# Recurrent mixing: value rows spread by transfers from DRAM, products and scans in SBUF

## The chip, the cores and the metric

The kernel runs on one core of one Trainium2 chip. The core has five engines that matter here: TensorE (PE, with its weight loads as PEld), VectorE (DVE), ScalarE (ACT), GpSimd (POOL) and SyncE (SP), which mostly issues DMAs. Each engine runs its own instruction stream in order, and the streams are tied together by semaphores. The metric is device time in microseconds (us) of one execution, as the median of several runs.

## What is computed

The reference runs four layers, one after the other, on 8 batch entries of 256 positions and 512 channels, all in float32: an attention block over two inputs (L0), a recurrent mixing block with 32 heads of 16 channels (L1), a decoder block with self-attention, cross-attention and an MLP (L2), and a non-local block of 1x1 convolutions (L3). The change is in L1, in its recurrence:

```python
def step(s, inp):
    k_l, v_l, w_l, r_l = inp
    a = k_l[..., :, None] * v_l[..., None, :]
    out = jnp.einsum('bhs,bhst->bht', r_l, faaaa * a + s)
    s_new = a + w_l[..., None] * s
    return (s_new, out)
```

Each head keeps a state of 16 x 16 numbers. At every position the state is multiplied by a decay w per key channel, the outer product of k and v is added, and the state is read out with r: multiplied and summed over the 16 key channels. The term with faaaa needs no state and is worked out apart (`bonus`). Ahead of the recurrence, k, v, r, w and a gate g come from projections of a mixed and normalised input; after it come a normalisation of each head, the gate, an output projection, and a second mixing block (`cm_` functions) of three projections.

## The kernel before

The program has four stretches: L0, the recurrent mixing of all eight entries, the self- and cross-attention of all entries, and the MLP with L3. The recurrent mixing is written in the class `Middle`. Its work is of two kinds.

The first kind is the recurrence, cut into 64 steps: 8 entries (b), 4 tiles of 128 channels (ct), 2 halves of the value channels (hf). In one step the 128 partitions hold 8 heads with 16 key channels each, and the free dimension holds 8 value channels of 256 positions each. The recurrence along the positions is one scan instruction over rows of 256; the decay of column 0 in each row is zero, so that a row starts from the initial state written there. A step consists of

- `spread` (L895): the value rows lie 128 channels to a partition. Eight matmuls with a selection matrix (`esel`, L902) copy the eight value rows of each head to the 16 partitions of that head, shifted by one position, into `vb`, which takes four banks of PSUM and has one buffer.
- `states` (L907): DVE copies the initial state to column 0 (L921), multiplies `vb` by k in two halves (L924), both in PSUM, and scans each half (L928) with the decays `w4`, which ACT writes for every second step (L912, L913). The scan reads `vb` from PSUM and `w4` from SBUF and writes a new SBUF tile `a`. POOL multiplies `a` by r into another tile `rs` (L933).
- `gather` (L936): eight matmuls with a selection matrix (`gsel`, L945) sum `rs` over the key channels into `yp`, one bank of PSUM; after the second half DVE adds the bonus (L951).

The second kind is everything else of the mixing, for the next entry and the one before: norms, projections, `mixed` (L762, whose DVE lines L777 read PSUM and whose POOL lines L784 add in SBUF), the shift (L737, with L741 and L744 on DVE), `head_norm`, `gated` (POOL L866), `gate` (DVE L876), `cm_` functions (POOL L971, L976, L995). These pieces are filler: the tables `steps` and `after` (L1199, L1210) give each function a due time in units of steps, eight to an entry, and `Filler.until` runs all that are due. The loop that joins both kinds is

```python
for n, at in enumerate(every):
    states(*at)
    fill.until(n + 0.95)
    if n:
        gather(*every[n - 1])
    fill.until(n + 0.99)
    if n + 1 < len(every):
        spread(*every[n + 1])
```

In this stretch only PE's stream is kept in the order of the program; the other engines' streams are ordered by the framework's scheduler, unless an instruction is pinned (`keep_in_program_order`). Matmul results of the filler go through a ring of PSUM banks (`mm`, L713), three in this stretch. Weights (1 MB for each of eight matrices, fetched anew for each entry by `load`, L809) come through a ring of SBUF buffers; their DMAs are issued by SP and wait there until the buffer is free.

Later lines that the text speaks of: `masked` (L1132) takes the attention tiles `pe`, from the same SBUF ring (tag "a") as the recurrence; `turn` (L1165) writes them to DRAM and reads them back with DMAs of 128 KB (L1177). In the MLP, sums of weights and activations are made on DVE and POOL, from SBUF to SBUF (L1351 to L1354 and L1360 to L1363), and results are combined from PSUM (L1407 to L1418).

Of the kernel before, what the change touches and what calls it, by code (L numbers as in the profile page):

```python
# [16 lines left out]
P = 128  # L17
# [76 lines left out]
def rows_of(halves):  # L94

    return [halves[k // 2][:, k % 2, :] for k in range(CT)]
# [20 lines left out]
def stage_l0(g, pools):  # L117
# [494 lines left out]

    "esel": (4, P), "gsel": (4, 32),
    "bfa": (CT, P),
# [7 lines left out]
class Middle:  # L622
# [62 lines left out]
    def plan(self):  # L685
        g, cp, wpool = self.g, self.cp, self.wpool
        nc, I = g.nc, g.I
        HS, NG = 16, 4
        w1, w2, w2g, d1, d2, s0, bones, bmean, cmean, esel, gsel, bfa = self.c.values()

# [28 lines left out]

        t_ = {}  # L720

        def fetch(b, tag, bufs):
            x = t_[tag, b] = wk.tile([P, ST, D], F32, tag=tag, name=tag, bufs=bufs)
            nc.sync.dma_start(out=x, in_=g.x1[b])

# [83 lines left out]
        def load(b, W):  # L809
            t_[W, b] = rows_of(g.weight(wpool, I["l1" + W + "T"], name=W))  # L810

# [80 lines left out]

        vbs, rss, w4s, yps = {}, {}, {}, {}

        def spread(b, ct, hf):  # L895

            v_ = t_["v", b]
            vb = vbs[b, ct, hf] = ps.tile([P, NG, 2, S], F32, tag="vb", name="vb", bufs=1)
            for j in range(2):
                for n in range(NG):  # L900
                    r = slice(32 * n, 32 * n + 32)
                    nc.tensor.matmul(  # L902
                        vb[:, n, j, 1:S], lhsT=esel[r, 2 * hf + j, :], rhs=v_[r, ct, 0 : S - 1],
                        start=True, stop=True,
                    )

        def states(b, ct, hf):  # L907


            if hf == 0:  # L910
                w4 = w4s[b, ct] = wk.tile([P, 4, S], F32, tag="w4", name="w4")
                nc.scalar.memzero(w4[:, :, 0:1])  # L912
                nc.scalar.activation(  # L913
                    w4[:, :, 1:S], t_["w", b][:, ct : ct + 1, 0 : S - 1].to_broadcast([P, 4, S - 1]),
                    AF.Exp, scale=-1.0,
                )
            w4 = w4s[b, ct]
            kb = t_["k", b][:, ct : ct + 1, 0 : S - 1].to_broadcast([P, 4, S - 1])
            rb = t_["r", b][:, ct : ct + 1, :].to_broadcast([P, 4, S])
            vb = vbs.pop((b, ct, hf)).rearrange("p n j l -> p (n j) l")  # L920
            nc.vector.tensor_copy(vb[:, :, 0], s0[:, b, ct, hf])  # L921
            for n2 in range(2):
                h = vb[:, 4 * n2 : 4 * n2 + 4, 1:S]
                nc.vector.tensor_tensor(h, h, kb, ALU.mult)  # L924
            rss[b, ct, hf] = []
            for n2 in range(2):
                a = wk.tile([P, 4, S], F32, tag="a", name="a", bufs=6)
                nc.vector.tensor_tensor_scan(  # L928
                    a.rearrange("p n l -> p (n l)"), w4.rearrange("p n l -> p (n l)"),
                    vb[:, 4 * n2 : 4 * n2 + 4, :].rearrange("p n l -> p (n l)"), 0.0, ALU.mult, ALU.add,  # L930
                )
                rs = wk.tile([P, 4, S], F32, tag="a", name="rs", bufs=6)
                nc.gpsimd.tensor_tensor(rs, a, rb, ALU.mult)  # L933
                rss[b, ct, hf].append(rs)

        def gather(b, ct, hf):  # L936
            if hf == 0:
                yps[b, ct] = ps.tile([P, S], F32, tag="y", name="yp", bufs=1)
                if ct % 2 == 0:
                    t_["y", b, ct // 2] = wk.tile([P, 2, S], F32, tag="y", name="y", bufs=2)  # L940
            yp = yps[b, ct]
            rs2 = rss.pop((b, ct, hf))
            for j in range(2):
                for n in range(NG):
                    nc.tensor.matmul(  # L945
                        yp[32 * n : 32 * n + 32, :], lhsT=gsel[:, 2 * hf + j, :],
                        rhs=rs2[n // 2][:, 2 * (n % 2) + j, :],
                        start=(hf == 0 and j == 0), stop=(hf == 1 and j == 1),
                    )
# [47 lines left out]
        def store(b):  # L997
            g.x2[b] = g.dram([P, ST, D], f"x2_{b}")
            nc.sync.dma_start(out=g.x2[b], in_=t_.pop(("xo", b)))


        HD, NH = 32, 4
        runs = [(pre, b) for pre in ("a_", "c_") for b in range(B)]

        pin = lambda ins: self.tc.keep_in_program_order(ins)

# [125 lines left out]
        def masked(i, ct, h2):  # L1132


            pe = t_["pe", i, ct, h2] = wk.tile([P, 2 * ST, S], F32, tag="a", name="pe", bufs=6)
            nmax = t_["nmax", i, ct, h2] = sm.tile([P, 2 * ST], F32, tag="nmax", name="nmax", bufs=4)
# [42 lines left out]
        def values(i, ct):  # L1179
# [92 lines left out]
        def loop(psums):  # L1272
            every = [(b, ct, hf) for b in range(B) for ct in range(CT) for hf in range(2)]
            bufs[0] = 3
            fill.until(-0.001)
            spread(*every[0])
            for n, at in enumerate(every):
                states(*at)
                fill.until(n + 0.95)
                if n:  # L1280
                    gather(*every[n - 1])
                fill.until(n + 0.99)
                if n + 1 < len(every):
                    spread(*every[n + 1])
            gather(*every[-1])
# [394 lines left out]
def host_layout(i):  # L1680
# [23 lines left out]
    vo = np.arange(D).reshape(CT, 8, 16).transpose(0, 2, 1).reshape(-1)  # L1704
    for nm in ("Wv", "Wg"):
        a["l1" + nm + "T"] = a["l1" + nm + "T"][:, vo]
    a["l1WoT"] = a["l1WoT"][vo]
    for nm in ("maa_w1", "decay_w1", "decay_w2"):
        a[nm] = L1[nm]
    w2 = L1["maa_w2"]  # L1710
# [4 lines left out]
    s0 = c[:, 2:18].reshape(B, CT, P, 4, 2, 2).transpose(2, 0, 1, 4, 3, 5)  # L1715
    a["s0"] = s0.reshape(P, B, CT, 2, 8)
    hs, th = np.arange(P) // 16, np.arange(P) % 8
    a["bones"] = (hs[:, None] == th[None, :]).astype(f)
# [3 lines left out]
    a["esel"] = np.stack([((t4 == t)[:, None] & (th[:, None] == hs[None, :])) for t in range(4)], 1).astype(f)  # L1722
    a["gsel"] = np.stack([((t4 == t)[None, :32] & (hs[:, None] == th[None, :32])) for t in range(4)], 1).astype(f)
    for nm in ("w_qkv", "w_ao", "w_q", "w_kv", "w_co", "w1", "w2"):
# [5 lines left out]
        "gn_w": L1["gn_w"][vo], "gn_b": L1["gn_b"][vo],  # L1730
        "bo": L0["bo"], "rwb": L0["r_w_bias"], "faaaa": L1["faaaa"],
        "a_ln_s": L2["ln1_s"], "a_ln_b": L2["ln1_b"], "c_ln_s": L2["ln2_s"], "c_ln_b": L2["ln2_b"],
# [36 lines left out]
```

## Time and profile before

| | us |
|---|---|
| median of 3 runs | 3414.48 (3413.72 to 3415.98) |
| the profiled execution | 3407.23 |
| its span in the profile | 3405.5 |
| first to last matmul of `spread` (L902) | 1377.2 to 2150.2 |
| PE busy over the span | 3197.5 (94%) |
| DVE busy | 2408.6 (71%) |
| ACT busy | 1591.4 (47%) |
| POOL busy | 1664.1 (49%) |

The profile is that of one execution, taken by the hardware profiler. A group line gives the source line, the engine, the operation, the tile written and the tiles read, and the number of instructions. A line's own view gives the shortest, median and longest duration in ns, and then the first and last start in us. Busy time counts an instruction from its recorded start to its end, so time in which a started instruction waits for something inside the chip is in it. Idle time is put down to whatever released the engine. "PEclk" or "clock" is the share of the full TensorE clock that was granted. A table by stretch gives, for each stretch of the span, its length, the busy time of PE, PEld, DVE, ACT and POOL with their numbers of instructions, the granted clock, the DMA engines' busy share and GB/s.

### The profile page before, as it was taken

Reading aid. Unit: us, or ns where it says so; the run is one execution under the profiler, and the core shown is the slowest. Engines: PE = TensorE matmul, PEld = TensorE weight load, DVE = VectorE, ACT = ScalarE, POOL = GpSimd, SP = SyncE. Lnnn points to the kernel's source line nnn. Section 1 sums busy time; section 2 is a strip of 40 time slices with the busy share of each in tenths; the row PEclk is TensorE's granted clock in tenths of the full one; section 3 lists DMA queues with packets and bytes.
Section 4 is the critical chain, followed back from the end, with each engine's and each line's share of the span. In section 5 each row is a group of like instructions: output and inputs, shape, how many; then the busy total and the mean of one; then the engine's idle time right before and its main releaser. Section 6 shows DMA issues by size and latency. Waiting matters only on the chain. (4 is left out here: it accounts for less than half of the span.)

```text
span 3405.5 us, 68751 instructions
## 1 busy us (share of the span) xinstructions
PE 3197.5 (94%) x26496; PEld 2271.7 (67%) x26496; DVE 2408.6 (71%) x4175; ACT 1591.4 (47%) x3983; POOL 1664.1 (49%) x1776
## 2 busy tenths in 40 slices
PE   8999999999999998889999998899989997899999
PEld 6777777777777765656666655555555553789996
DVE  4666666666666664787787887667868886677771
ACT  3555555555555553224334333566656664323223
POOL 6633233333333232455666665444434444688872
PEclk9999999999999998989999999899999998999999
DMA  7666566656657542312323233366777777400002
GB/s 269 228 202 198 189 192 194 204 184 196 207 176 223 173 128 69 112 55 87 106 93 111 95 101 101 106 231 238 252 247 256 267 258 245 164 1 1 1 13 87
DMA packets 273141, 533.08 MB, mean 157 GB/s; under 512 B 25056, under 2 KB 147312, under 8 KB 268720
## 3 DMA queue, kind: packets, MB, share of 16 engines
q1 hardware_dynamic: 251616, 456.48, 41.3%
q10 hardware_dynamic: 20528, 70.39, 5.4%
q8 instruction: 211, 3.46, 0.4%
q0 software_dynamic: 672, 1.81, 0.2%
q14 instruction: 114, 0.93, 0.1%
HBM read 411.15 MB, written 117.44 MB: 155 GB/s over the span
## 5 line engine op out<-in xcount | busy, mean ns | idle before, releaser
L391 POOL TENSOR_SCALAR pe<-pe,rinv 128x512 f32<-128x512 f32 x256 | 176.9, 691 | 609.1 <-DVE rinv L390 603.9
L368 DVE TENSOR_REDUCE nmax<-sp 128x2 f32<-128x1024 f32 x256 | 308.8, 1216 | 177.2 <-PE sp L363 177.2
L933 POOL TENSOR_TENSOR rs<-a,r 128x1024 f32<-128x1024 f32 x128 | 302.6, 2380 | 254.1 <-DVE a L928 223.1
L1161 POOL TENSOR_SCALAR pe<-pe,rinv 128x256 f32<-128x256 f32 x512 | 235.3, 478 | 349.6 <-DVE rinv L1159 345.2
L1151 ACT ACTIVATE pe<-pe,nmax 128x256 f32<-128x256 f32 x512 | 255.1, 499 | 210.5 <-DVE nmax L1142 204.4
L377 ACT ACTIVATE pe<-sp,nmax 128x512 f32<-128x512 f32 x512 | 347.0, 683 | 11.2
L403 DVE STREAM_TRANSPOSE pt<-pe 128x1024 f32<-128x1024 f32 x256 | 312.6, 1231 | 24.2 <-POOL pe L391 15.3
L432 PE MATMUL av<-pt,vr 32*64 32x256 f32 x8192 | 263.9, 389 | 36.9 <-issue 28.7
L928 DVE TENSOR_TENSOR_SCAN a<-w,vb 128x1024 f32<-128x1024 f32 x128 | 287.3, 2275 | 4.8
L432 PEld LDWEIGHTS av<-pt,vr 32*64 32x64 f32 x8192 | 209.1, 136 | 104.1 <-issue 58.7
L363 PE MATMUL sp<-k,q 64*64 64x512 f32 x2048 | 266.6, 612 | 5.6 <-ACT pe L377 5.6
L373 ACT ACTIVATE nmax<-nmax 128x2 f32<-128x2 f32 x256 | 51.8, 203 | 399.0 <-DVE nmax L368 398.9
L303 PEld LDWEIGHTS gp<-t,ws 128*128 128x128 f32 x1512 | 184.8, 192 | 30.1 <-ACT pe L396 11.1
L303 PE MATMUL gp<-t,ws 128*128 128x128 f32 x1512 | 202.2, 277 | 1.7 <-POOL ws L289 1.4
L396 ACT ACTIVATE pe<-pe,rinv 128x512 f32<-128x512 f32 x256 | 182.6, 729 | 41.2 <-DVE rinv L390 41.2
L924 DVE TENSOR_TENSOR vb<-vb,k 128x1020 f32<-128x1020 f32 x128 | 157.2, 1228 | 4.4
L1171 DVE STREAM_TRANSPOSE dt<-pe 128x1024 f32<-128x1024 f32 x128 | 155.6, 1216 | 4.3 <-POOL pe L1161 4.3
L902 PE MATMUL vb<-v,mconstc 32*128 32x255 f32 x1024 | 98.7, 441 | 57.2 <-DVE a L928 56.4
L1447 ACT ACTIVATE h<-h,pvec 128x256 f32<-128x256 f32 x124 | 55.9, 500 | 201.8 <-DVE h L1416 164.6
L390 DVE RECIPROCAL rinv<-ssum 128x2 f32<-128x2 f32 x256 | 41.1, 160 | 146.8 <-ACT pe L377 146.8
L1190 PE MATMUL cp<-pt,av 128*32 128x256 f32 x1024 | 93.3, 403 | 45.6 <-DMA pt<-pt 44.8
L455 PEld LDWEIGHTS op<-av_sb,wo 128*128 128x128 f32 x512 | 93.3, 192 | 55.9 <-issue 27.5
(311 smaller groups left out, 7582.8 us busy)
## 6 DMA issues: line engine op xcount, KB each, us to landing
pt<-dt ACTq DMA_DIRECT2D x128, 512.0 KB, 3.7
pt<-pt SPq DMA_DIRECT2D x512, 128.0 KB, 3.4
ws<-sqk SPq DMA_DIRECT2D x110, 512.0 KB, 5.0
wqk<-in_wqk_dram SPq DMA_DIRECT2D x70, 512.0 KB, 5.4
vr<-v SPq DMA_DIRECT2D x128, 256.0 KB, 4.7
ws<-sv SPq DMA_DIRECT2D x56, 512.0 KB, 4.8
wv<-in_wv_dram SPq DMA_DIRECT2D x36, 512.0 KB, 5.0
v<-vT SPq DMA_DIRECT2D x64, 256.0 KB, 2.5
```

The source lines that it names most:

```text
L303: nc.tensor.matmul(out[:, hf * P : (hf + 1) * P], lhsT=w[n](hf, k), rhs=a[n](hf, k), start=k == 0, stop=k == ST - 1,)
L363: nc.tensor.matmul(sp[a * 64 : (a + 1) * 64, h, :], lhsT=qs[b, 2 * un + a][r, ic], rhs=ks[b, 2 * un + a][r, :], start=True, stop=True,)
L368: nc.vector.tensor_reduce(nmax, sp, AX.X, ALU.max, negate=True)
L377: nc.scalar.activation(pe[:, h, :], sp[:, h, :], AF.Exp, bias=nmax[:, h : h + 1], scale=1.0 / DH ** 0.5, accum_out=ssum[:, h : h + 1],)
L391: nc.gpsimd.tensor_scalar(pe[:, 0, :], pe[:, 0, :], rinv[:, 0:1], 1.0, ALU.mult, ALU.mult)
L396: nc.scalar.mul(pe[:, 1, :], pe[:, 1, :], rinv[:, 1:2])
L403: nc.vector.transpose(pts[b, un][:, it], pe)
L432: nc.tensor.matmul(av[r][h * DH : (h + 1) * DH], lhsT=vr[rows_, kb, h * DH : (h + 1) * DH], rhs=pt[rows_, :, h, 32 * kb : 32 * kb + 32], s ...
L928: nc.vector.tensor_tensor_scan(a.rearrange("p n l -> p (n l)"), w4.rearrange("p n l -> p (n l)"), vb[:, 4 * n2 : 4 * n2 + 4, :].rearrange( ...
L933: nc.gpsimd.tensor_tensor(rs, a, rb, ALU.mult)
L1151: pin(nc.scalar.activation(pe[:, r, :], pe[:, r, :], AF.Exp, bias=nmax[:, r : r + 1], scale=-1.0, accum_out=ssum[:, r : r + 1],))
L1161: pin(nc.gpsimd.tensor_scalar(pe[:, r, :], pe[:, r, :], rinv[:, r : r + 1], 1.0, ALU.mult, ALU.mult))
```

## The change

`spread` no longer uses TensorE. A new function `v_store` writes the value rows of an entry to DRAM in two halves, as soon as they are projected, and `spread` reads them back with eight DMAs a step, each of which broadcasts one row set to 16 partitions. `vb` moves from PSUM to SBUF, with four buffers. The product and the scan work in place in `vb`, and so does the readout by POOL; the tiles `a` and `rs` are gone. The initial state is copied by ACT. `spread` is issued ahead of `states` of the step before, and for the first step 1.45 steps ahead. The filler's ring of PSUM banks grows from three to six in this stretch, `yp` gets two buffers. The heads' channels are ordered on the partitions as 16 channels of 8 heads (the weights' columns, decay, initial state and selection matrices are permuted on the host accordingly). The DMAs that SP issues in this stretch are pinned to the order of the program. In the attention the `pe` tiles of two half steps share one tile with four buffers, in place of six single ones. The descriptor scratch for DMAs issued by POOL is set to 8192.

```diff
         def fetch(b, tag, bufs):
             x = t_[tag, b] = wk.tile([P, ST, D], F32, tag=tag, name=tag, bufs=bufs)
-            nc.sync.dma_start(out=x, in_=g.x1[b])
+            pin(nc.sync.dma_start(out=x, in_=g.x1[b]))
...
-            t_[W, b] = rows_of(g.weight(wpool, I["l1" + W + "T"], name=W))
+            t_[W, b] = rows_of(g.weight(wpool, I["l1" + W + "T"], name=W, pin=pin))
...
+        def v_store(b, c2):
+            if c2 == 0:
+                t_["vd", b] = g.dram([P, CT, S], f"v{b}")
+            c = slice(2 * c2, 2 * c2 + 2)
+            pin(nc.sync.dma_start(out=t_["vd", b][:, c, :], in_=t_["v", b][:, c, :]))
 
         def spread(b, ct, hf):
 
-            v_ = t_["v", b]
-            vb = vbs[b, ct, hf] = ps.tile([P, NG, 2, S], F32, tag="vb", name="vb", bufs=1)
-            for j in range(2):
-                for n in range(NG):
-                    r = slice(32 * n, 32 * n + 32)
-                    nc.tensor.matmul(
-                        vb[:, n, j, 1:S], lhsT=esel[r, 2 * hf + j, :], rhs=v_[r, ct, 0 : S - 1],
-                        start=True, stop=True,
-                    )
+            rows = t_["vd", b].rearrange("(g f h) c s -> h f c g s", f=2, h=2 * NG)
+            vb = vbs[b, ct, hf] = wk.tile([P, 2 * NG, S], F32, tag="a", name="vb", bufs=4)
+            for h in range(2 * NG):
+                pin(nc.sync.dma_start(
+                    out=vb[h :: 2 * NG, :, 1:S], in_=rows[h, hf, ct, :, 0 : S - 1].partition_broadcast(HS)
+                ))
 
         def states(b, ct, hf):
...
-            vb = vbs.pop((b, ct, hf)).rearrange("p n j l -> p (n j) l")
-            nc.vector.tensor_copy(vb[:, :, 0], s0[:, b, ct, hf])
-            for n2 in range(2):
-                h = vb[:, 4 * n2 : 4 * n2 + 4, 1:S]
-                nc.vector.tensor_tensor(h, h, kb, ALU.mult)
-            rss[b, ct, hf] = []
-            for n2 in range(2):
-                a = wk.tile([P, 4, S], F32, tag="a", name="a", bufs=6)
+            vb = vbs[b, ct, hf]
+            nc.scalar.copy(vb[:, :, 0], s0[:, b, ct, hf])
+            halves = [vb[:, NG * n2 : NG * n2 + NG, :] for n2 in range(2)]
+            for h in halves:
+                nc.vector.tensor_tensor(h[:, :, 1:S], h[:, :, 1:S], kb, ALU.mult)
+            for h in halves:
+                flat_ = h.rearrange("p n l -> p (n l)")
                 nc.vector.tensor_tensor_scan(
-                    a.rearrange("p n l -> p (n l)"), w4.rearrange("p n l -> p (n l)"),
-                    vb[:, 4 * n2 : 4 * n2 + 4, :].rearrange("p n l -> p (n l)"), 0.0, ALU.mult, ALU.add,
+                    flat_, w4.rearrange("p n l -> p (n l)"), flat_, 0.0, ALU.mult, ALU.add,
                 )
-                rs = wk.tile([P, 4, S], F32, tag="a", name="rs", bufs=6)
-                nc.gpsimd.tensor_tensor(rs, a, rb, ALU.mult)
-                rss[b, ct, hf].append(rs)
+                nc.gpsimd.tensor_tensor(h, h, rb, ALU.mult)
 
         def gather(b, ct, hf):
             if hf == 0:
-                yps[b, ct] = ps.tile([P, S], F32, tag="y", name="yp", bufs=1)
+                yps[b, ct] = ps.tile([P, S], F32, tag="y", name="yp", bufs=2)
...
-            pe = t_["pe", i, ct, h2] = wk.tile([P, 2 * ST, S], F32, tag="a", name="pe", bufs=6)
+            if h2 == 0:
+                t_["pes", i, ct] = wk.tile([P, 4 * ST, S], F32, tag="a", name="pe", bufs=4)
+            pe = t_["pe", i, ct, h2] = t_["pes", i, ct][:, 2 * ST * h2 : 2 * ST * h2 + 2 * ST, :]
...
-            (5.5, kvrg, "v", 0), (6.1, kvrg, "v", 1), (6.3, kvrg, "r", 0), (7.1, kvrg, "r", 1),
+            (5.5, kvrg, "v", 0), (6.1, kvrg, "v", 1), (5.8, v_store, 0), (6.45, v_store, 1), (6.3, kvrg, "r", 0), (7.1, kvrg, "r", 1),
...
-            bufs[0] = 3
+            bufs[0] = 6
+            fill.until(-1.45)
+            spread(*every[0])
             fill.until(-0.001)
-            spread(*every[0])
             for n, at in enumerate(every):
+                if n + 1 < len(every):
+                    spread(*every[n + 1])
                 states(*at)
...
-                if n + 1 < len(every):
-                    spread(*every[n + 1])
...
-    nc = _bacc.Bacc("TRN2", target_bir_lowering=False, num_devices=1)
+    nc = _bacc.Bacc("TRN2", target_bir_lowering=False, num_devices=1, dynamic_dma_scratch_size=8192)
```

More of the change, by code (lines that the diff above doesn't have):

```diff
@@ L611 @@
     "bones": (P,), "bmean": (P,), "cmean": (P,),
-    "esel": (4, P), "gsel": (4, 32),
+    "gsel": (4, 32),
     "bfa": (CT, P),
@@ L688, in plan @@
         HS, NG = 16, 4
-        w1, w2, w2g, d1, d2, s0, bones, bmean, cmean, esel, gsel, bfa = self.c.values()
+        w1, w2, w2g, d1, d2, s0, bones, bmean, cmean, gsel, bfa = self.c.values()
         class sm:
@@ L720, in plan @@
         t_ = {}
+        pin = lambda ins: self.tc.keep_in_program_order(ins)
         def fetch(b, tag, bufs):
             x = t_[tag, b] = wk.tile([P, ST, D], F32, tag=tag, name=tag, bufs=bufs)
-            nc.sync.dma_start(out=x, in_=g.x1[b])
+            pin(nc.sync.dma_start(out=x, in_=g.x1[b]))
         def norm(b):
@@ L890, in out_proj @@
             nc.vector.tensor_tensor(xb[:, st, :], xb[:, st, :], op, ALU.add)
[L893 to L905 removed]
+        vbs, w4s, yps = {}, {}, {}
+        def v_store(b, c2):
[3 more added lines that the diff above has]
+            pin(nc.sync.dma_start(out=t_["vd", b][:, c, :], in_=t_["v", b][:, c, :]))
+        def spread(b, ct, hf):
+            rows = t_["vd", b].rearrange("(g f h) c s -> h f c g s", f=2, h=2 * NG)
[4 more added lines that the diff above has]
+                ))
         def states(b, ct, hf):
@@ L941, in gather @@
             yp = yps[b, ct]
-            rs2 = rss.pop((b, ct, hf))
+            rs = vbs.pop((b, ct, hf))
             for j in range(2):
@@ L945, in gather @@
                     nc.tensor.matmul(
-                        yp[32 * n : 32 * n + 32, :], lhsT=gsel[:, 2 * hf + j, :],
-                        rhs=rs2[n // 2][:, 2 * (n % 2) + j, :],
+                        yp[32 * n : 32 * n + 32, :], lhsT=gsel[:, 2 * j + hf, :], rhs=rs[:, 2 * n + j, :],
                         start=(hf == 0 and j == 0), stop=(hf == 1 and j == 1),
@@ L998, in store @@
             g.x2[b] = g.dram([P, ST, D], f"x2_{b}")
-            nc.sync.dma_start(out=g.x2[b], in_=t_.pop(("xo", b)))
+            pin(nc.sync.dma_start(out=g.x2[b], in_=t_.pop(("xo", b))))
         HD, NH = 32, 4
         runs = [(pre, b) for pre in ("a_", "c_") for b in range(B)]
-        pin = lambda ins: self.tc.keep_in_program_order(ins)
         def at_fetch(i):
@@ L1704, in host_layout @@
     vo = np.arange(D).reshape(CT, 8, 16).transpose(0, 2, 1).reshape(-1)
-    for nm in ("Wv", "Wg"):
+    for nm in ("Wr", "Wk", "Wv", "Wg"):
         a["l1" + nm + "T"] = a["l1" + nm + "T"][:, vo]
@@ L1709, in host_layout @@
         a[nm] = L1[nm]
+    a["decay_w2"] = a["decay_w2"][:, vo]
     w2 = L1["maa_w2"]
@@ L1713, in host_layout @@
     a["sh"] = np.ascontiguousarray(c[:, 0:2].reshape(B, 2, CT, P).transpose(3, 1, 2, 0))
-    s0 = c[:, 2:18].reshape(B, CT, P, 4, 2, 2).transpose(2, 0, 1, 4, 3, 5)
+    s0 = c[:, 2:18].reshape(B, CT, 8, 16, 4, 2, 2).transpose(3, 2, 0, 1, 6, 4, 5)
     a["s0"] = s0.reshape(P, B, CT, 2, 8)
-    hs, th = np.arange(P) // 16, np.arange(P) % 8
-    a["bones"] = (hs[:, None] == th[None, :]).astype(f)
+    th = np.arange(P) % 8
+    a["bones"] = (th[:, None] == th[None, :]).astype(f)
     a["bmean"] = (th[:, None] == th[None, :]).astype(f) / 16
@@ L1721, in host_layout @@
     t4 = np.arange(P) // 8 % 4
-    a["esel"] = np.stack([((t4 == t)[:, None] & (th[:, None] == hs[None, :])) for t in range(4)], 1).astype(f)
-    a["gsel"] = np.stack([((t4 == t)[None, :32] & (hs[:, None] == th[None, :32])) for t in range(4)], 1).astype(f)
+    a["gsel"] = np.stack([((t4 == t)[None, :32] & (th[:, None] == th[None, :32])) for t in range(4)], 1).astype(f)
     for nm in ("w_qkv", "w_ao", "w_q", "w_kv", "w_co", "w1", "w2"):
@@ L1730, in host_layout @@
         "gn_w": L1["gn_w"][vo], "gn_b": L1["gn_b"][vo],
-        "bo": L0["bo"], "rwb": L0["r_w_bias"], "faaaa": L1["faaaa"],
+        "bo": L0["bo"], "rwb": L0["r_w_bias"], "faaaa": L1["faaaa"].reshape(-1)[vo], "time_decay": L1["time_decay"][vo],
         "a_ln_s": L2["ln1_s"], "a_ln_b": L2["ln1_b"], "c_ln_s": L2["ln2_s"], "c_ln_b": L2["ln2_b"],
```

## The prediction

> **What bounds the kernel now.** I cut the span with the table of busy time by stretch, using the first and last starts of the mixing lines. The first 1377 us are the opening attention block and the lead-in, 1377.2 to 2170.5 the recurrent mixing, then 740 us of attention and 495 us of MLP. The change touches the second stretch.
>
> ```profile
> 1657.70:1757.90 100.20, 96.02 (x565) 62.12 (x564) 81.49 (x91) 37.65 (x69) 61.09 (x30) 0.97 0.29 97
> 1377.20:2170.50 793.30, 719.06 (x4301) 469.74 (x4300) 637.04 (x684) 282.09 (x508) 476.21 (x224) 0.95 0.27 88
> ```
>
> The columns are length, then busy PE, PEld, DVE, ACT and POOL, clock, DMA share, GB/s. The first row is one batch entry in the steady part: of 100.2 us PE is busy 96.0, DVE 81.5, POOL 61.1. PE sets the pace, DVE is close behind, and **DVE and POOL work at the same time**: 81.5 + 61.1 = 142.6 us of work in 100.2 us. Whether that overlap survives is the question of this change. Next, the views of single lines: durations as min/median/max in ns.
>
> ```profile
> L902 PE MATMUL vb<-v,mconstc x1024: 373/373/791, 1377.2 to 2150.2; 32*128 32x255 f32 x171
> L924 DVE TENSOR_TENSOR vb<-vb,k x128: 1220/1228/1229, 1378.6 to 2159.8; 128x1020 f32<-128x1020 f32 x128
> L928 DVE TENSOR_TENSOR_SCAN a<-w,vb x128: 2259/2279/2289, 1382.2 to 2163.3; 128x1024 f32<-128x1024 f32 x128
> L933 POOL TENSOR_TENSOR rs<-a,r x128: 2337/2357/2821, 1384.7 to 2165.8; 128x1024 f32<-128x1024 f32 x128
> ```
>
> Products (L924) and scans (L928) never vary. Each reads one tensor from PSUM (vb) and one from SBUF. Now four DVE lines in the same stretch and in the MLP:
>
> ```profile
> L777 DVE SCALAR_TENSOR_TENSOR x_maa_w<-mp,pvec,sx x32: 441/473/485, 1312.0 to 2003.2; 128x256 f32<-128x256 f32 x32
> L744 DVE SCALAR_TENSOR_TENSOR xxx<-sx,pvec,xs x32: 457/472/2575, 1277.3 to 1979.5; 128x256 f32<-128x256 f32 x32
> L1416 DVE TENSOR_TENSOR h<-proj,s x31: 406/424/426, 2933.0 to 3318.9; 128x256 f32<-128x256 f32 x31
> L1352 DVE TENSOR_TENSOR ws<-w,ws x32: 677/1750/1759, 2918.5 to 3309.4; 128x512 f32<-128x512 f32 x32
> ```
>
> L777 and L1416 have one operand in PSUM and are constant. L744 and L1352 read **two tensors from SBUF** and stretch to 2575 and 1759 ns. The timeline shows what L744 waits for:
>
> ```profile
> 1571.74 4.99 POOL L933 TENSOR_TENSOR rs<-a,r 128x1024 f32<-128x1024 f32 x2 [5.61 <-DVE a L928]
> ...
> 1574.06 3.35 DVE L744 SCALAR_TENSOR_TENSOR xxx<-sx,pvec,xs 128x256 f32<-128x256 f32 x3
> ```
>
> POOL's pair ends at 1576.73. Of the three L744, two take their usual 0.46 and one 2.6: it began just after POOL's second multiply and ended some 0.3 us after it. The pair took 4.99 instead of 2 x 2.36, so POOL also waited 0.27 for the first L744. Scans ran beside POOL's multiply undisturbed. So a DVE instruction with two SBUF tensors and a POOL instruction take turns, in both directions.
>
> The Trainium skill, page "SBUF — State Buffer", section "SBUF: two separate sides", says the same: GpSimd and a DVE instruction with two SBUF inputs share one port pair, locked for a whole instruction. Its section claims no partial overlap. By that the sum below would be its upper form, 950 us for the stage.
>
> **The change part by part.**
>
> *Removed from PE:* 1024 spread matmuls, 98.7 us busy in the groups of the page, plus 62.9 us in which PE waited for "DVE a" before them. PSUM for other matmuls grows from 3 to 6 banks and yp from 1 to 2. This saves time only while PE sets the pace. Per steady entry PE would need 96.0 - 98.7/8 = 84 us.
>
> *Removed from DVE:* 64 small copies (L921), 10.3 us, which go to ACT. ACT is busy 282 of 793 us and has room; 64 copies at about 0.2 us (the 128x4 ACT copies of L912) are 13 us. Cost nothing; if ACT came late, the scan would wait for it.
>
> *Products and scans move to SBUF.* Length: the nearest all-SBUF row is L741, 128x1024, 1.212 us at least, so 1.21 against 1.228: 2 us in all. Page "VectorE: DVE Perf Modes", section on the errata, gives PSUM sources 62 cycles more, which would be about 8 us for 128 products. The rows (0.677 for L1352, 0.680 for the PSUM L846, both 128x512) show no such gap. The scan I keep at 2.275 us.
>
> *The overlap.* After the change product and scan read vb and k, or vb and w4, all in SBUF. They join the class that takes turns with POOL. No row shows a scan with two SBUF tensors, so its cost is bounded by no waiting (L928 as it is) and full waiting (L744, L1352). I take full waiting: these are the nearest rows with two SBUF operands. Sum over 1377 to 2170, undisturbed durations:
> - DVE: products 128 x 1.21 = 155; scans 287; L741 7 x 1.22 = 9; L744 28 x 0.47 = 13; L876 15 x 0.69 = 10. Together 474 us.
> - POOL: all 476 us of it, of which the readouts (L933) are 303.
>
> That is **950 us that must take turns, in a stage that lasts 793**. How tightly do turns pack? The MLP tells. From 2960 to 3290 the DVE ran 102 two-SBUF instructions of 128x512 (0.675) and 66 of 128x256 (0.43), POOL 127 of 512 columns (1.26) and 131 of 256 (0.72): 69 + 28 + 160 + 94 = 351 us in 330. Part of each instruction lies outside its turn: from 512 to 1024 columns DVE grows by 0.535 us, so 0.14 is fixed; POOL from 256 to 512 by 0.55, so 0.17 is fixed. If all of that hides, 306 x 0.14 + 224 x 0.17 = 81 us goes, leaving 869. With the MLP's ratio, 950 x 330/351 = 893. I take 893.
>
> What leaves the turn unused comes on top. DVE's other work (637 - 157 - 287 - 26 - 15 - 9 - 10 = 133 us, 2.1 per step) falls after the second scan, as built; there POOL has two readouts pending, so it is covered. The wait of L876 for ACT's y is 48 us over 15 now; POOL fills most, I leave 2 us each, 30. The last readout pair no longer runs beside a scan: 2. Start: store v (2.5 us landing in v<-vT), then eight loads; step 0's are issued 1.45 steps ahead, so I allow 5. Stage: 893 + 37 = **930 us, +137**.
>
> *PE afterwards:* 719 - 99 = 620 us of 930. The clock may fall; from 2850 to 2900, PE busy 61%, it was 0.76 against 0.95 here. 620 x 0.95/0.76 = 775, still under 930.
>
> *Transfers.* Each step adds 8 DMAs of 130,560 bytes, 128 rows of 1020 bytes each. The nearest row is pt<-pt (L1177): 128 KB in 1 KB rows, 602 ns of SP per issue, 3.4 us to landing. SP: 8 x 0.6 = 4.8 us of a 14.5 us step. Engines: q1 between 2250 and 2850 moved 74,885 packets in 48.1% of 16 x 600 us, 62 ns each; 1024 x 62/16 = 4 us a step, beside 0.27 x 12.4 = 3.3 us of the present traffic. With four vb tiles, the buffer of step n+1 is free when step n-3 is gathered, two steps ahead. The loads queue on SP behind weight loads that wait for PE (up to 35 us in the waits of SP), but PE runs about a step ahead of DVE now that it is idle a third of the time. Hidden: 0 us, and each us by which a landing is late would cost up to 64.
>
> *Rest:* attention's pe tiles in pairs (8 halves for 6) and the smaller descriptor scratch change no duration there: 0 within some us.
>
> Sum: 3407.2 (profiled run; span 3405.5) + 137 = 3544; the median shown lies 7.3 above that run: 3414.5 + 137 = **3552 us**.
>
> **The rivals.**
> - *No turns (faster).* If neither product nor scan with two SBUF tensors waited, what remains is PE 84 and DVE 80 per entry plus DVE's waits of some 10: 84 to 92 for 100.2. Eight entries: -65 to -130, 3285 to 3350. It decides if products stay at 1.21 us beside a running readout. For it: PE is the bound and loses 12%. Against: L744, L1352. Chance 0.07.
> - *Only products take turns (same or a little faster).* Scans overlap the readouts as now; turns sum to 950 - 287 = 663 < 793, so they do not bind. DVE loses about 1.5 us a step, 12 an entry: 80 + 12 + 5 = 97 for 100.2. 3385 to 3425. Against: the scan reads two tensors like the others. Chance 0.05.
> - *Transfers set the pace (much slower).* A step of 14.5 us has 16 x (14.5 - 3.3) = 179 us of engine time, 175 ns for each of 1024 packets. Above that, loads bind; at three times 62 ns the step is 15.2, at four times 19: +6.8 x 64 = +435, 3850. Against: pt<-pt. For: rows start one element off, and 16 partitions read the same row. Chance 0.05.
> - *The forecast:* both take turns. Chance 0.83.
>
> **How the numbers follow.** The forecast's own ends: packing 869 with 10 us unused gives +86, 3500; 950 unhidden with 80 unused gives +237, 3652. The three others hold 0.17, under 2 in 10, so the range is these ends, with 10 us more below: 3490 to 3652. Changes under 0.2% (7 us) can't be told from none. Faster: 0.07 + 0.03 of the products' case = 0.10; same 0.02; slower 0.83 + 0.05 = 0.88.
>
> **What would show it.** Right: in the changed profile products and scans range from 1.2 and 2.3 up to 3.5 and 4.6 us, as L744 does now; readouts stretch as well; PE in the mixing falls to about two thirds busy; a steady entry takes about 118 us; DVE plus POOL busy exceeds the stage by far, since waiting counts as busy. Wrong: scans constant at 2.28 while readouts run (the second rival); DVE waiting for DMA before the product (the third); a gain with PE still at 95% (the first). The attention and MLP stretches should keep 740 and 495 us.

## The result, and the profile after

The changed kernel takes **4095.0 us** (median of 4 runs, 4091.5 to 4098.6) against 3414.1 us for the kernel before in the same session: ratio 1.2008, 95% interval 1.1986 to 1.2030. The forecast was 3552, with 3652 as the upper end. The direction was right; the loss is 681 us where 138 were forecast.

The head of the page after, first the span and the busy times, then the slices of PE's clock:

```profile
span 4096.7 us, 68034 instructions
...
PE 3352.2 (82%) x25472; PEld 2313.5 (56%) x25472; DVE 2432.5 (59%) x4111; ACT 1614.9 (39%) x4055; POOL 1784.7 (44%) x1775
...
PEclk9999999999998766767777777676999999899999
```

The low clock marks the mixing stage, slices 14 to 28. The table by stretch (length, busy PE, PEld, DVE, ACT, POOL, clock, DMA share, GB/s), from the first product to the last readout (to within 3 us) and for 740 us behind it:

```profile
1399.40:2850.00 1450.60, 862.36 (x3236) 499.77 (x3236) 658.24 (x618) 302.52 (x574) 592.54 (x221) 0.71 0.37 98
```

```profile
2851.00:3591.00 740.00, 684.98 (x3797) 399.99 (x3798) 564.64 (x1656) 436.96 (x1378) 318.66 (x594) 0.95 0.70 241
```

Nearly the whole loss lies in the mixing: of the 691 us between the two profiled executions, 663 lie between the start of the first product and the end of the last readout (1452 us in place of 790), 22 ahead of them and 6 behind. No engine sets the pace there: PE is busy 59%, DVE 45%, POOL 41%. DVE and POOL together are busy 1251 us, less than the stage lasts, so even work that never overlapped would not fill it. The attention behind it keeps its length within 6 us: from the last readout to the MLP's first L1352 pass 753 us before and 759 after.

The lines of the mixing (durations min/median/max in ns; the products, scans and readouts that were L924, L928 and L933):

```profile
L928 DVE TENSOR_TENSOR vb<-vb,k x128: 1208/1215/3353, 1400.9 to 2841.2; 128x1020 f32<-128x1020 f32 x128
L931 DVE TENSOR_TENSOR_SCAN vb<-w,vb x128: 2257/2276/4373, 1403.2 to 2846.7; 128x1024 f32<-128x1024 f32 x128
L934 POOL TENSOR_TENSOR vb<-vb,r x128: 2333/2346/4325, 1405.7 to 2851.0; 128x1024 f32<-128x1024 f32 x128
```

All three now range up to the forecast's stretched values, but their medians are the undisturbed ones. Turns exist; they are not what fills the stage. The waits over 1400 to 2850 (total, times, longest):

```profile
PE yp L945 <- POOL vb L934: 572.7, 119, 15.8
...
DVE y L950 <- PE yp L945: 164.9, 31, 6.5
```

PE idles 588 us in the stage and 573 of them are waits of the gather for POOL's readouts. One step in the timeline (start, length, what it did; in brackets the idle time before it and what ended that):

```profile
1907.66 1.06 PE L945 MATMUL yp<-vb,mconstc 128*32 128x256 f32 x12 [0.49 <-POOL vb L934]
1908.65 1.09 PE L83 MATMUL ln_tp<-ident,xn 128*128 128x128 f32 x8
...
1911.31 1.23 DVE L742 TENSOR_TENSOR sx<-xs 128x1024 f32<-128x1024 f32 x1 [8.15 <-ACT xs L88]
...
1913.03 3.62 PE L818 MATMUL proj<-x_maa_g,Wg 128*128 128x256 f32 x16
...
1916.69 0.60 ACT L831 ACTIVATE g<-proj 128x512 f32<-128x512 f32 x1 [2.19 <-PE proj L818]
...
1917.32 0.69 DVE L832 SCALAR_TENSOR_TENSOR g<-g,proj 128x512 f32<-128x512 f32 x1 [3.08 <-ACT g L831]
1917.92 2.35 DVE L928 TENSOR_TENSOR vb<-vb,k 128x1020 f32<-128x1020 f32 x2
1920.18 4.47 DVE L931 TENSOR_TENSOR_SCAN vb<-w,vb 128x1024 f32<-128x1024 f32 x2
1922.69 6.40 POOL L934 TENSOR_TENSOR vb<-vb,r 128x1024 f32<-128x1024 f32 x2 [15.08 <-issue]
...
1929.15 1.92 PE L945 MATMUL yp<-vb,mconstc 128*32 128x256 f32 x12 [1.23 <-POOL vb L934]
...
1931.12 0.42 DVE L950 TENSOR_TENSOR y<-yp,hv 128x256 f32<-128x256 f32 x1 [6.46 <-PE yp L945]
1931.49 2.35 DVE L928 TENSOR_TENSOR vb<-vb,k 128x1020 f32<-128x1020 f32 x2
```

Read it as one chain. A gather ends at 1908.7; PE then does the filler (transposes, projections); ACT and DVE finish a piece of it at 1918.0; only then does DVE start the next products, though nothing in their data needed that piece. Scans, readouts and the next gather follow, and DVE's y (L950) stands in front of the products after that. Each step waits for PE's filler and each filler waits for the step. The products hardly wait for their transferred rows. The groups of the page (busy, mean ns | idle before, releaser) and its list of DMA issues (KB, median us to landing):

```profile
L928 DVE TENSOR_TENSOR vb<-vb,k 128x1020 f32<-128x1020 f32 x128 | 205.5, 1646 | 1.2 <-DMA fWk<-in_l1fWkT_dram 0.9
...
vb<-v SPq DMA_DIRECT2D x512, 127.5 KB, 4.6
```

DVE waited 1.2 us before its products in the whole stage. (In POOL's waits a readout is at times put down to the DMA of its rows, 211 us in all; the products that came two instructions earlier on the same rows had not waited, so the label is not the cause.)

The reason stands in DVE's instruction order, which the framework's scheduler sets. In the kernel before, DVE does the same pieces behind the product of step 16:

```profile
1556.49 2.49 DVE L924 TENSOR_TENSOR vb<-vb,k 128x1020 f32<-128x1020 f32 x2
...
1565.03 2.49 DVE L924 TENSOR_TENSOR vb<-vb,k 128x1020 f32<-128x1020 f32 x2
1568.15 1.23 DVE L741 TENSOR_TENSOR sx<-xs 128x1024 f32<-128x1024 f32 x1 [0.63 <-ACT xs L88]
...
1577.33 0.67 DVE L831 SCALAR_TENSOR_TENSOR g<-g,proj 128x512 f32<-128x512 f32 x1
1577.93 0.41 DVE L951 TENSOR_TENSOR y<-yp,hv 128x256 f32<-128x256 f32 x1
...
1578.45 2.49 DVE L924 TENSOR_TENSOR vb<-vb,k 128x1020 f32<-128x1020 f32 x2
```

The pieces between two products in both kernels, in the steady part (number: step; sx, xxx and g belong to the filler of step 16, y to the gather of step 15; the step shown above is the same one, an entry later):

```
before: product 15 | (nothing)  | product 16 | sx, xxx, g, y | product 17
after:  sx, xxx, g | product 15 | y          | product 16    | maa_w, maa_k ...
```

PE's order of filler and gathers is the same in both: filler 15, gather 14, filler 16, gather 15. In the kernel before, the filler's pieces follow the product of the same step. In the changed kernel the pieces of filler 16 stand *ahead* of product 15; PE does filler 16 only after gather 14, which needs the readouts of step 14. That closes the loop.

### The profile page after: what moved, and what is told of

It reads as the page before. It is cut to its first block, busy times and chain, and to the rows that moved or that the text cites. A ratio compares the mean times of both kernels' runs of the same rounds, so it can differ in the third digit from the quotient of the medians.

```text
span 4096.7 us, 68034 instructions
## 1 busy us (share of the span) xinstructions
PE 3352.2 (82%) x25472; PEld 2313.5 (56%) x25472; DVE 2432.5 (59%) x4111; ACT 1614.9 (39%) x4055; POOL 1784.7 (44%) x1775
## 5 line engine op out<-in xcount | busy, mean ns | idle before, releaser
L945 PE MATMUL yp<-vb,mconstc 128*32 128x256 f32 x1024 | 179.7, 602 | 580.1 <-POOL vb L934 580.1
L934 POOL TENSOR_TENSOR vb<-vb,r 128x1024 f32<-128x1024 f32 x128 | 402.3, 3163 | 495.0 <-DMA vb<-v 210.8
L945 PEld LDWEIGHTS yp<-vb,mconstc 128*32 128x32 f32 x1024 | 46.4, 144 | 697.6 <-POOL vb L934 665.2
L931 DVE TENSOR_TENSOR_SCAN vb<-w,vb 128x1024 f32<-128x1024 f32 x128 | 288.2, 2292 | 0.0
L928 DVE TENSOR_TENSOR vb<-vb,k 128x1020 f32<-128x1020 f32 x128 | 205.5, 1646 | 1.2 <-DMA fWk<-in_l1fWkT_dram 0.9
```

Of the source, the lines that this page charges most:

```text
L928: nc.vector.tensor_tensor(h[:, :, 1:S], h[:, :, 1:S], kb, ALU.mult)
L931: nc.vector.tensor_tensor_scan(flat_, w4.rearrange("p n l -> p (n l)"), flat_, 0.0, ALU.mult, ALU.add,)
L934: nc.gpsimd.tensor_tensor(h, h, rb, ALU.mult)
L945: nc.tensor.matmul(yp[32 * n : 32 * n + 32, :], lhsT=gsel[:, 2 * j + hf, :], rhs=rs[:, 2 * n + j, :], start=(hf == 0 and j == 0), stop=(hf ...
```

## The experiments

My theory after this reading: **order** costs most, turns come next, transfers little. Rivals: turns alone (as forecast), or transfers. Runs are compared with the kernel before in the same session (3406 to 3411 us).

**1. VectorE in program order.**

```diff
-    with stack, tc.manual_schedule(engines={mybir.EngineType.PE}):
+    with stack, tc.manual_schedule(engines={mybir.EngineType.PE, mybir.EngineType.DVE}):
         ln0 = middle.run(pools)
```

> The changed kernel with one thing altered: in the recurrent mixing VectorE's stream, too, is kept in the order of the program. Theory A (order): the scheduler put VectorE's part of the filler of step n+1, and the addition after gather n, ahead of the product of step n; so each step waits for the step before, through readout, gather and TensorE. With the order mended only the turns of VectorE and GpSimd are left, and the stage should last about 930 us as forecast: 3500 to 3650 us in all. Theory B (turns alone cost the 680 us): little changes, above 3950. Theory C (late transfers): little changes, above 3950.

Measured 3677.1, ratio 1.0776 (1.0760 to 1.0793): 418 us less than the changed kernel, from an edit of DVE's order alone, and a little above the range expected.

**2. No turns, scheduler's order.** The decays (two rows of four, so four scans of 512 elements) and the k row are put in PSUM; no product or scan has two SBUF inputs any more. The PSUM for it comes from the filler (four banks in place of six) and from `yp` (one buffer).

```diff
-                w4 = w4s[b, ct] = wk.tile([P, 4, S], F32, tag="w4", name="w4")
+                w2_ = ps.tile([P, 2, S], F32, tag="wk", name="w2_", bufs=2)
+                kp = ps.tile([P, S], F32, tag="kp", name="kp", bufs=1)
...
+                nc.scalar.copy(kp, t_["k", b][:, ct, :])
```

> The changed kernel, the scheduler's order kept, with the decays and the row of k in PSUM, so that neither product nor scan reads two tensors from SBUF; each scan is cut in two of 512 columns; the filler has four PSUM banks, yp one. Theory A: the chain of the step stays, only the first readout now runs beside the second scan, some 2.2 us of a 22.7 us step: 64 x 2.2 = 140 us less, 3900 to 4000. Theory B: the 680 us go, 3300 to 3450. Theory C: no change, about 4100.

3976.9, ratio 1.1659 (1.1642 to 1.1677): 118 less than the changed kernel. Turns alone don't explain the loss; 567 us stay without them.

**3. Both.** Edit 1 and edit 2 together.

> Both at once: VectorE in the order of the program, decays and k in PSUM. Theory A, with the turns as forecast: neither cost is left, PE or DVE at 84 to 92 us per entry set the pace, and the two more scans a step add 0.3 us: 3300 to 3380. Theory B: as the run before, since the order does nothing. Theory C: about 4100.

3584.1, ratio 1.0498 (1.0477 to 1.0519). A miss: some 170 us that neither DVE's program order nor turns explain. One part of it is this experiment's own doing: k's PSUM row has one buffer, and ACT waits for DVE's products to free it (75 us from 1400 to 2300 in its trace).

**4. Transfers alone.** The kernel before, with v's stores and the 512 broadcast transfers added, into a tile that nobody reads.

```diff
+                if n + 1 < len(every):
+                    dspread(*every[n + 1])
                 states(*at)
```

> The kernel before, with the value rows also stored to DRAM and read back by the same 512 DMAs into an SBUF tile that nobody reads; spreading and the rest as before. It measures what the transfers cost by contention on SP and the DMA engines alone. Theories A and B: 0 to 20 us more, 3410 to 3435. Theory C: hundreds of us more, because weights arrive late.

3448.7, ratio 1.0101 (1.0079 to 1.0122): +39 us, more than the 0 to 20 expected. The waits of its trace tell where, from 1400 to 2300:

```profile
PE ln_tp L83 <- DVE xn L68: 29.3, 5, 11.2
PE ln_tp L83 <- POOL axn L1051: 26.6, 4, 13.6
```

The kernel before has no such waits. The inputs of the next entry, and of attention, are fetched by the same SP queue, and the fetches now come later: that of the fourth entry is issued at 1521.2 us (1443.7 before), that of attention's first input at 2149.6 (2071.3). Run 15 tests this for attention. For the entries it is not the fetch that PE waits for: from 1400 us on DVE waits for it in neither kernel, but the scheduler, which ordered DVE's stream anew, put the norm of the next entry just ahead of sx, where the kernel before has its statistics five steps earlier. So run 4 holds some cost of order too, and 39 us is not the price of the transfers alone.

**5. and 6. All four engines in program order,** with turns and without them.

```diff
-    with stack, tc.manual_schedule(engines={mybir.EngineType.PE}):
+    with stack, tc.manual_schedule(engines=every):
```

> The changed kernel with TensorE, VectorE, ScalarE and GpSimd all in the order in which the program writes them (in the changed kernel only TensorE is; in the first order run TensorE and VectorE). That run took 3677 us. Theory (the order of the engines' streams closes each step of the recurrence into a serial chain, and the turns of VectorE and GpSimd come on top): the ScalarE and GpSimd streams hold the rest of the order's cost, so this run should lie at 3500 to 3580 us, about what the forecast had from the turns alone. Rival (the rest is turns and transfers, and ScalarE's order costs nothing): 3660 to 3690, as before.

> The same with all four engines in the program's order, and in addition the decays (two rows of four, so four scans of 512 elements in place of two of 1024) and the k row in PSUM, so that no VectorE product or scan has both inputs in SBUF. The version of this with only TensorE and VectorE in program order took 3584 us. Theory: with neither turns nor a closed chain TensorE sets the pace again, without the spread: 3330 to 3430 us, the products at 1.2 us and the scans at 1.2 us for 512. Rival (ScalarE's order costs nothing; the 170 us left over are transfers or scan starts): 3570 to 3600.

3735.5 (1.0965, 1.0948 to 1.0981) and 3610.9 (1.0598, 1.0580 to 1.0616). Both worse than with ACT and POOL left to the scheduler: the theory's simple form ("program order is the cure") falls.

**7. Control: the kernel before, all in program order.**

> A control: the kernel before with all four engines in the program's order. Theory: the order in which its VectorE, ScalarE and GpSimd streams stand lets TensorE run ahead already, so pinning them to the program's order changes little: 3410 to 3470 us. If program order by itself were worth hundreds of us in any kernel, this would fall to under 3300, and the gains of the order runs would say nothing of the change.

3601.0, ratio 1.0568 (1.0546 to 1.0590). My expectation for the control (3410 to 3470) falls too, and the control accounts for most of 5 and 6: program order by itself costs the kernel before 190 us, and its partner, run 6, lies only 10 us above it. So "program order" was the wrong yardstick; the order in which the kernel before runs is 190 us better.

**8. Products into PSUM.** Run 1 with the product written to PSUM and the scan reading it there: the product still has two SBUF inputs, the scan one. The four banks for it leave the filler three, `yp` one.

```diff
-                nc.vector.tensor_tensor(h[:, :, 1:S], h[:, :, 1:S], kb, ALU.mult)
+                nc.vector.tensor_tensor(q[:, :, 1:S], h[:, :, 1:S], kb, ALU.mult)
...
-                    flat_, w4.rearrange("p n l -> p (n l)"), flat_, 0.0, ALU.mult, ALU.add,
+                    flat_, w4.rearrange("p n l -> p (n l)"), q.rearrange("p n l -> p (n l)"), 0.0, ALU.mult, ALU.add,
```

> The first order run (TensorE and VectorE in program order, 3677 us) with the products written to PSUM and the scan reading them there and writing SBUF: the scan then has one input in SBUF (the decays) and takes no turns, the product still has two (the transferred rows and k). Theory (a VectorE instruction takes turns with GpSimd when both its inputs are in SBUF): scans constant at about 2.26 us, products still at 1.2 to 3.5 us; GpSimd's readouts, which mostly meet scans, fall to about 2.33 us; most of the 93 us that the turns cost between 3677 and 3584 goes: 3590 to 3630 us. Rival (the output in SBUF counts as well): scans still stretched, 3660 to 3690.

3648.9, ratio 1.0709 (1.0690 to 1.0728), only 28 us under run 1 and above the 3590 to 3630 expected. The time says little, since this kernel's products wait 135 us for ACT's copy into the single PSUM tile; the lines (products, then scans) say it plainly:

```profile
L930 DVE TENSOR_TENSOR pv<-vb,k x128: 1218/1229/3366, 1408.6 to 2409.1; 128x1020 f32<-128x1020 f32 x128
...
L933 DVE TENSOR_TENSOR_SCAN vb<-w,pv x128: 2260/2274/2289, 1411.2 to 2412.7; 128x1024 f32<-128x1024 f32 x128
```

Two SBUF inputs: stretched to 3366, although the output goes to PSUM. One input in PSUM: constant, although the output goes to SBUF. It is the inputs that count.

**9. and 10. A fair order for both kernels.** The kernel before with PE and DVE in program order, and the same with norms, gates and POOL's product of the bonus put up to two steps earlier.

```diff
-            (-3.9, fetch, "xi", 1), (-1, norm), (-0.4, normed), (0.2, norm_T), (0.5, shift), (1.1, lora),
+            (-4.9, fetch, "xi", 1), (-3, norm), (-1.88, normed), (0.2, norm_T), (0.25, shift), (1.1, lora),
...
-            (21, cm_norm), (21.6, cm_normed), (21.9, cm_norm_T), (22, cm_mix),
+            (19.85, cm_norm), (19.98, cm_normed), (21.9, cm_norm_T), (22, cm_mix),
```

> The kernel before with TensorE and VectorE in the program's order: the fair partner of the first order run (3677 us) and of its version without turns (3584). With all four engines in program order the kernel before took 3601. Theory: the program's order is itself a poor one for either kernel, and the order in which the kernel before runs is worth 150 to 190 us: 3560 to 3610. Rival (only the program's order of ScalarE and GpSimd is poor): 3410 to 3450.

> The kernel before with TensorE and VectorE in program order, but with norm statistics, normalisation, gates and the GpSimd product of the bonus put up to two steps earlier in the program, so that VectorE's stream stands about as in the kernel before; TensorE's stream is the same. Theory: 3410 to 3470. If the due times matter little: as the run without them, 3560 to 3610.

3469.0 (1.0177, 1.0151 to 1.0203) and 3410.5 (1.0008, 0.9994 to 1.0021). DVE's program order costs the kernel before 63 us, between the two expectations, and the due times give most of them back.

**11. and 12. The same due times in the changed kernel,** with turns and without.

> The changed kernel with TensorE and VectorE in program order and the same earlier due times: VectorE's stream then stands as the forecast assumed it, with the order of the kernel before. Theory (order, then turns): about the forecast's figure, 3510 to 3600; products and scans stretched as in the first order run (means 1.8 and 2.9 us). Rival (the program's order was not the rest): 3650 to 3690.

> The same with the decays and the k row in PSUM, so that no product or scan has both inputs in SBUF. Theory (with neither turns nor a poor order, what is left is the saving on TensorE against the transfers' collisions): 3340 to 3440, near the kernel before. Rival: 3560 to 3590.

3674.8 (1.0782, 1.0757 to 1.0807) and 3566.5 (1.0463, 1.0437 to 1.0489). Next to nothing gained. My reading, which run 13 then tests: with DVE's stream mended, the scheduler's order of the *other* streams holds the stage. Run with turns, waits from 1450 to 2250:

```profile
ACT k L834 <- PE proj L818: 198.9, 12, 28.9
POOL y L869 <- ACT sq L865: 131.0, 12, 15.4
```

POOL stands 131 us at y (L869), a piece of an older entry, with readouts queued behind it; the square it waits for is on ACT, behind copies that wait for PE.

**13. The very order of the kernel before, on all engines.** Every instruction of DVE, ACT and POOL in the mixing gets an edge (order only, no wait) to the one that stands before it in the kernel before. Left to the scheduler: the 64 state copies that moved to ACT, and the norms of the first three entries. The fetch of an entry goes three steps earlier in SP's stream.

```diff
+            for engine, places in ORDER.items():
+                mine = [i for k, i in said if k.split(":")[1] == engine]
+                for a, b in zip(places, places[1:]):
+                    self.tc.add_manual_dep(
+                        mine[b], mine[a].name,
...
-            (-3.9, fetch, "xi", 1), (-1, norm), (-0.4, normed), (0.2, norm_T), (0.5, shift), (1.1, lora),
+            (-6.9, fetch, "xi", 1), (-1, norm), (-0.4, normed), (0.2, norm_T), (0.5, shift), (1.1, lora),
```

> The changed kernel with the instructions of VectorE, ScalarE and GpSimd held, through the mixing stage, in the very order in which they stand in the kernel before (a list of places taken from that kernel's streams; TensorE's is the same anyway; the fetch of the next batch is put three steps earlier in SyncE's stream, so that statistics can stand as early as they did). The order is then no part of the difference any more. Theory (what was left in the run with earlier due times was the order of ScalarE and GpSimd): turns and transfers remain, 3500 to 3580, the forecast's figure. Rival (something of the change itself costs the rest): 3640 to 3690.

**3621.6**, ratio 1.0618 (1.0598 to 1.0638). 473 us of the loss are gone, with the order and the earlier fetch. The time lies 42 us above the range of the theory and below that of the rival; but for the pieces left to the scheduler, what is left is no matter of order on DVE, ACT and POOL. The mixing of this run, from the first product to the last readout, and its lines:

```profile
1392.70:2370.00 977.30, 706.60 (x3240) 429.49 (x3240) 841.27 (x623) 284.07 (x569) 666.25 (x224) 0.84 0.55 145
```

```profile
L935 DVE TENSOR_TENSOR vb<-vb,k x128: 1203/1554/3400, 1392.7 to 2360.0; 128x1020 f32<-128x1020 f32 x128
L938 DVE TENSOR_TENSOR_SCAN vb<-w,vb x128: 2258/2281/4429, 1396.1 to 2363.4; 128x1024 f32<-128x1024 f32 x128
L941 POOL TENSOR_TENSOR vb<-vb,r x128: 2332/2518/4357, 1398.6 to 2367.7; 128x1024 f32<-128x1024 f32 x128
```

This is the picture that the forecast drew: DVE and POOL busy 1508 us in 977, PE 72%, the medians of product and readout themselves stretched.

**14. The same without turns.** Decays and k in PSUM as in run 2, two buffers each; the filler keeps three banks, `yp` one buffer.

> The same with the decays (two rows of four, four scans of 512 elements) and the k row in PSUM, two buffers of each, so that neither products nor scans take turns with GpSimd. Theory: TensorE sets the pace again and is spared the spread, against the transfers' 39 us: 3320 to 3420, as fast as the kernel before or faster. Rival: 3530 to 3580, as the earlier runs without turns.

**3425.7**, ratio 1.0040 (1.0026 to 1.0054). That is just above the range. Turns cost 196 us in this order (run 13 less run 14; the edit's smaller PSUM rings and its four scans are in this figure). In the poorer orders the same kind of edit was worth less: 118 us (run 2), 93 (run 1 less run 3), 125 (run 5 less run 6), 108 (run 11 less run 12). Products and readouts range as in the kernel before:

```profile
L938 DVE TENSOR_TENSOR vb<-vb,kp x128: 1185/1208/1221, 1403.6 to 2181.4; 128x1020 f32<-128x1020 f32 x128
```

```profile
L945 POOL TENSOR_TENSOR vb<-vb,r x128: 2334/2360/2821, 1409.5 to 2187.3; 128x1024 f32<-128x1024 f32 x128
```

The price of four scans for two is small: 4 x 1.20 us against 2 x 2.28 a step, 15 us in the stage, beside PE. Steady entries now run faster than before. From the first to the last of the last six entries' lora matmuls, which frame the same work in both kernels (L753 before, L761 here):

```profile
L753 PE MATMUL tp<-xxx,mconstb x96: 379/379/797, 1479.2 to 1982.3; 128*128 128x256 f32 x48, 128*32 128x256 f32 x48
```

```profile
L761 PE MATMUL tp<-xxx,mconstb x96: 379/379/794, 1496.3 to 1978.4; 128*128 128x256 f32 x48, 128*32 128x256 f32 x48
```

482.1 us against 503.1 for five entries. What is won there is lost at the ends of the stage: the frame starts 17 us later than before, and though it ends 4 us earlier the last readout comes 21 us later. At the start DVE waits 20 us for a DMA before the first product; at the end it waits for attention's first input, which SP fetches behind the transfers:

```profile
2094.56 1.29 DVE L58 BATCH_NORM_STATS2 ln_stats<-axi 128x6 f32<-128x512 f32 x2 [15.82 <-DMA axi<-x]
```

**15. and 16. Looking for a gain.** Run 14 with attention's fetches two steps earlier, then the transfers two steps ahead as well.

```diff
-                (-5.98, at_fetch), (-4.6, at_norm), (-4.3, at_normed), (-3.6, at_norm_T), (-3.98, at_inputs), (-2.6, at_mask),
+                (-8.2, at_fetch), (-4.6, at_norm), (-4.3, at_normed), (-3.6, at_norm_T), (-3.98, at_inputs), (-2.6, at_mask),
```

```diff
             spread(*every[0])
+            spread(*every[1])
...
-                if n + 1 < len(every):
-                    told(f"spread.{n + 1}", spread, *every[n + 1])
+                if n + 2 < len(every):
+                    told(f"spread.{n + 2}", spread, *every[n + 2])
```

> The run without turns in the order of the kernel before (3426 us), with attention's fetches of its inputs put two steps earlier in SyncE's stream. Its trace shows 28.8 us of VectorE waiting for them at the end of the mixing stage. Theory (steady batches there take 96.4 us against 100.6 before; what is lost is at the stage's end): 3385 to 3410, a little under the kernel before. Rival (that wait is covered): 3420 to 3430.

> The last run (3405 us, 0.9985 of the kernel before) with the eight transfers of a step issued two steps ahead in place of one. Its trace shows VectorE waiting 35 us for transferred rows, 20 of them at the start of the stage behind a weight load. Theory (late landings are what is left): 3375 to 3400. Rival (those waits are covered, or move to the next load): 3400 to 3410.

3405.2, ratio 0.9985 (0.9971 to 0.9999), and 3412.5, 1.0015 (1.0000 to 1.0030). The first takes off 20 us and ends within 0.2% of the kernel before, no gain that can be told; the second gives nothing: DVE's products wait 38 us for DMAs in both, and 7 us of waiting for attention's input come back. No version beat the kernel before clearly.

## Why the prediction was wrong, point by point

The loss, taken apart step by step: **order 473** (4095.0 to 3621.6, the earlier fetch included), **turns 196** (3621.6 to 3425.7), **the rest 17** (3425.7 against 3409.1 for the kernel before in that session: the transfers against what PE is spared). The forecast had 0, 137 and 0. The split depends on the way: with the turns taken out first, they are worth 118 and the order 551.

- **The step that failed** is the sentence on DVE's other work: it "falls after the second scan, as built; there POOL has two readouts pending, so it is covered". I looked at where these pieces stand beside DVE's own instructions and priced them as busy time (2.1 us a step). What they *wait for* I did not follow: in the changed stream they belong to a filler that PE starts only after the gather of the step before. The same holds for "PE runs about a step ahead of DVE now": PE's gathers need products which, in DVE's stream, stand behind pieces of PE's own filler. The order is fixed when the kernel is built, so no duration was needed to see it; following one step's waits around the loop would have shown it closed. Runs 1 and 13 show the price, 418 and 473 us. Why the scheduler chose this order is not shown by any run.
- **The overlap** was right as a mechanism: both products and scans take turns, to 3.4 and 4.4 us, and run 8 shows that the inputs decide it. Its size was too low, 930 us where the stage of run 13 takes 977. The packing was not the reason. By the starts and ends in run 13's trace, a POOL instruction or one of DVE's with two SBUF inputs is in progress for 899 of the 977 us (the term said 893), and none for 78, where I had left 37 unused. In these 78 DVE is at its other work for 38 (put at 0, as "covered"), waits 21 for attention's first input and 13 for ACT's y before the gate (30 allowed). The Trainium skill, page "SBUF — State Buffer", section "SBUF: two separate sides", has it that the shared port pair is held for the whole instruction. On recorded durations that would make 950 us; run 13's 899 are 51 less, so the recorded durations overlap a little.
- **The first rival** ("no turns") is what run 14 built. It was put at 3285 to 3350 and came at 3426. PE is indeed spared, but an entry falls only from 100.6 to 96.4 us, not to 84 to 92, and the stage's ends give that back.
- **Removed from PE, small copies, length of product and scan:** as priced. Products 1.208 to 1.215 us undisturbed, scans 2.276, copies 0.20; PE's saved work bought nothing while it wasn't the pace. Of the 62.9 us that PE was said to wait before the spread, its matmuls waited 56.4, the rest being its weight loads; the sum didn't use it. PE's busy time did not fall to 620 us, since the clock fell too: 862 at 0.71 in the changed kernel, 707 at 0.84 in run 13, where 620 x 0.95/0.84 gives 701. How much of the 473 us is this slower clock inside the chain is not shown.
- **Transfers "0 us":** in the changed kernel the landing was hidden (median 4.6 us after issue, where the nearest row had 3.4, and 0.6 us of SP each). In runs 14 to 16, where DVE isn't late itself, its products wait 33 to 38 us for DMAs, 20 of them at the stage's start. And the queue delays other loads: fetching attention's inputs earlier took off 20 us (run 15). Run 4's +39 us holds such delays and some order. The third rival is out. The start was too small as well: from the lead-in's last DVE line (L482) to the first product pass 36 us before and 49 after, 14 more where I allowed 5.
- **Signs:** the ranges of product, scan and readout came as said, and attention's 740 us within 6. An entry of 118 us did not (943.5 us from first to last in the frame above, that is some 189 an entry; run 13 has 125), nor did "DVE plus POOL busy exceeds the stage by far": 1251 in 1451. That was the sign that told turns from a serial chain.

## What to carry to other kernels

Where a scheduler orders the streams, a change of one producer can reorder the others: before pricing anything, read the new order and follow one step's waits around the loop, asking of each instruction ahead of the critical one which engine feeds it, and behind what. Moving operands from PSUM to SBUF can cost more than the matmuls it removes, because here a DVE instruction with two SBUF inputs took turns with GpSimd's (196 us in this kernel's own order, against 99 us of matmuls removed). To tell order from everything else, force the old order onto the new kernel; "program order" is no neutral yardstick until the old kernel has been run in it too.

## What the runs showed of the hardware that was not expected

A scan with one PSUM input and its output in SBUF is undisturbed by GpSimd (2260 to 2289 ns in run 8), one with both inputs in SBUF is not (to 4429 in run 13). Taking turns was nearly, but not quite, one after the other: what is some 950 us undisturbed was in progress for 899 us of run 13's stage. And PE's granted clock fell further than the 0.76 allowed for: to 0.71 over the stage in which PE was busy 59% of the time, 0.84 where it was busy 72% (run 13), against 0.95 at 91% before.
